# A transformer block in one core: first token tiles of batch 2 and of the MLP prepared inside attention, other tiles on GpSimd's queue

## The chip, the core and the metric

The kernel runs on one core of a Trainium2 chip. The core has a matrix engine (TensorE, PE in the profile; PEld are its weight loads), a vector engine (VectorE, DVE), an engine for functions (ScalarE, ACT), a general one (GpSimd, POOL) and one that only issues transfers (SyncE, SP). Transfers can be issued by SP, ACT and POOL. Each engine works its own instructions off in order and waits at semaphores for the others. The metric is the device time of one execution in microseconds (us); lower is better.

## What is computed

One block of a conditioned transformer on x of 2 batches x 2048 tokens x 576 features, 16 heads of 36, MLP width 2304, all in float32:

```
mod = silu(c) @ w_ada + b_ada                  # six rows of 576 for each batch
xn  = layernorm(x, 1e-6) * (1 + sc_msa) + sh_msa
q, k, v = xn @ w_qkv + b_qkv, by head; q, k = layernorm over the head
o   = softmax(q k^T / sqrt(36)) v
x   = x + g_msa * (o @ w_proj + b_proj)
xn2 = layernorm(x, 1e-6) * (1 + sc_mlp) + sh_mlp
out = x + g_mlp * (gelu(xn2 @ w1 + b1) @ w2 + b2)
```

## The kernel before

With small gains of the head norms (as here) the branch `block_of_small` runs. TensorE's instructions keep the order in which they are written, over the whole branch. Elsewhere a scheduler of the language places the instructions of each engine, and may pull one forward if its inputs are there; inside `tc.manual_schedule(engines=...)` the named engines keep the written order for the instructions of that section. Tiles of a pool have a number of buffers, and a new tile waits until the old one in its buffer is no longer read.

The stages, for each of the two batches:

- **Input stage** (`inputs`): 16 token tiles of 128. A tile is loaded, normalised over its row (`rows_normed`: statistics and normalisation on VectorE, square root on ScalarE), transposed in 32x32 squares on VectorE into the one buffer `squares`, stored as four transfers into a DRAM tile `turned` of 576 x 128 (`tile_turned`), and loaded back with features on partitions (`turned_loaded`: one transfer of 512 features, two of the last 64). ScalarE applies the modulation (`turned_modulated`), GpSimd forms the rest part. `product` multiplies by the weights: four whole chunks of 128 features (L1025) and one of 64 in two rounded parts (L1027). VectorE adds biases and norms the heads. VectorE is in written order here.
- **Attention** (`attend`): 8 head pairs p x 4 query blocks qb x 4 key groups g, 128 steps of about 6 us. A step has score products (L1117), exponentials on ScalarE (L1121) and, one step later, value products (L1130) that VectorE adds up in `ot` (L1176, L1178). `finish` sends the row sums through DRAM, divides, and stores into `qo` (L1155). A dictionary `hooks` puts other work at a step (p, qb, g). The PSUM has eight banks `b`, handed out in turn.
- **Projection** (`outputs`): the PSUM is laid out anew as four tiles `s` of two banks. Four groups of four token tiles: whole chunks of the first two tiles, the last chunk for all four (L423), whole chunks of the other two (L412). VectorE evicts each tile times the gate (L1227) and adds the residual (L1234), which goes to `x1_dram`. The dictionary `between` puts other work before tile t.
- **MLP**, after both batches: first products in a seven-product scheme over 8 token blocks and 9 feature steps (L1494, L1508), gelu, hidden values to DRAM; then the second products (L1645).

In the kernel before, the two first tiles of batch 2 are turned from `between` of the first projection, and the first five of the MLP from that of the second, both with transfers on ACT's queue; the sums and rest parts of w1 are made there too (L1409 to L1412 on VectorE, L406, L407 and L1405 on GpSimd). The second projection and the MLP are one section with VectorE in written order. Other token tiles use SP's queue, but MLP loads use GpSimd's. The w1 loads stand on SP behind the last `qo` stores of attention. The buffer of the transposed tile and the order around it:

```
squares = xs["pool"].tile([P, C], F32, name="squares", bufs=1)
nc.vector.transpose(squares, xt[:, :C])
...
with tc.manual_schedule(engines={mybir.EngineType.DVE, mybir.EngineType.Pool}):
    attend(b, att, hooks)
```

Of the kernel before, what the change touches and what calls it, by code (L numbers as in the profile page):

```python
# [31 lines left out]
def dit_block(  # L32
# [368 lines left out]
    def weight_parts(dst, src, subtract=None):  # L401

        if subtract is None:
            nc.vector.tensor_copy(dst[0:64], src)
        else:
            subtract.tensor_copy(dst[0:64], src)  # L406
        (subtract or nc.vector).tensor_tensor(dst[64:128], src, dst[0:64].bitcast(F32), ALU.subtract)  # L407
# [350 lines left out]
    def block_of_small():  # L758
# [99 lines left out]
        def input_weights(then=lambda t: None):  # L858
            pool, close = opened("wq")
            wq = pool.tile([P, FULL, 3 * C], F32, name="wq")  # L860
            wq4 = pool.tile([P, 3 * C], F32R, name="wq4")
            bq = pool.tile([P, 3 * C], F32, name="bq")
            for f0, n in ((0, HALF), (HALF, HALF), (C, C), (2 * C, C)):
                f = slice(f0, f0 + n)
                nc.sync.dma_start(out=wq[:, :, f], in_=w_qkv[0:512, f].rearrange("(k p) f -> p k f", p=P))
                if f0 == HALF:
                    nc.sync.dma_start(out=bq[0:64, :], in_=w_qkv[512:576, :])
                    weight_parts(wq4, bq[0:64, :])
                if f0 == C:
                    then(1)  # L870
                    nc.sync.dma_start(out=bq, in_=b_qkv.partition_broadcast(P))
                    then(2)
            return (wq, wq4, bq), close
# [12 lines left out]
        def tile_turned(xt, queue):  # L886

            rows_normed(xs["pool"], xt, repeated=False)
            squares = xs["pool"].tile([P, C], F32, name="squares", bufs=1)
            nc.vector.transpose(squares, xt[:, :C])  # L890
            xs["count"] = xs.get("count", 0) + 1
            turned = dram.tile([C, P], F32, name=f"turned{xs['count']}")
            by_square = turned.rearrange("(k d) (g j) -> g d k j", d=SQ, j=SQ)
            for g in range(P // SQ):
                queue.dma_start(
                    out=by_square[g], in_=squares[g * SQ : (g + 1) * SQ, :].rearrange("p (k j) -> p k j", j=SQ)
                )
            return turned

        def turned_loaded(dst, cols, turned, queue):  # L900

            full, _, tail = dst
            queue.dma_start(out=full[:, :, cols], in_=turned[0:512, :].rearrange("(k p) n -> p k n", p=P))
            for r0 in (0, 64):
                queue.dma_start(out=tail[r0 : r0 + 64, :], in_=turned[512:576, :])

        def turned_modulated(dst, cols, which, b):

            full, _, tail = dst
            for k in range(FULL):  # L910
                part = full[:, k, cols]
                nc.scalar.activation(part, part, AF.Identity, **affine(which, k, b))  # L912
            last_modulated(dst, cols, tail, which, b)
# [24 lines left out]
        def inputs(b, weights, work, xnt, rows, loaded):  # L938
# [75 lines left out]
            def next_rows(t):  # L1014
                return tile_turned(loaded.pop(0), nc.sync) if loaded else input_turned(b, t, nc.sync)

            def product(w, xnt):

                ps = s_tile()
                full, parts, _ = xnt  # L1020
                for a in range(2):
                    f = slice(w * C + a * HALF, w * C + (a + 1) * HALF)
                    out_a = ps[:, a, :HALF]
                    for k in range(FULL):
                        nc.tensor.matmul(out_a, full[:, k, :], wq[:, k, f], start=k == 0, stop=False)  # L1025
                    for i in range(2):
                        nc.tensor.matmul(out_a, parts[:, i, :], wq4[:, f], start=False, stop=i == 1)  # L1027
                return ps
# [17 lines left out]
            for t in range(NT - 2):  # L1046
# [4 lines left out]
                if not turning:  # L1051
                    ahead = input_loaded(rows, nc.sync)
                q = product(0, xnt)
                k = product(1, xnt)
                if turning:
                    ahead = second_by_feature(rows)
                else:
                    input_modulated(b, ahead)
# [13 lines left out]
            for t in range(NT - 2, NT):  # L1072
                both = work.tile([P, 2 * C], F32, name="both", bufs=3)
                if t + 1 < NT:
                    ahead = input_loaded(rows, nc.sync)
# [124 lines left out]

        def residual_begun(b, t):
# [77 lines left out]
        for b in range(B):  # L1279
# [44 lines left out]
            }  # L1324
            if b == 0:
# [6 lines left out]
            with tc.manual_schedule(engines={mybir.EngineType.DVE, mybir.EngineType.Pool}):  # L1332
                attend(b, att, hooks)
# [4 lines left out]
            if b + 1 < B:  # L1338
                weights, close_weights = input_weights()
                between = {  # L1340
                    6: [lambda: opening.update(rows=input_turned(b + 1, 0, nc.scalar))],
                    8: [lambda: opening.update(xnt=input_loaded(opening["rows"], nc.scalar))],
                    10: [lambda: opening.update(rows=input_turned(b + 1, 1, nc.scalar))],
                    12: [lambda: input_modulated(b + 1, opening["xnt"])],
                }
                outputs(b, wp, between, spare)
                xnt, rows = opening["xnt"], opening["rows"]
# [47 lines left out]
        nc.sync.dma_start(out=last_rows, in_=w1[512:576, :].rearrange("p (a f) -> p a f", a=2))  # L1395
        for i, (k, f) in enumerate(((0, 0), (0, 1), (1, 0), (1, 1))):
# [3 lines left out]
            )  # L1400
        left, right = last_rows[:, 0], last_rows[:, 1]
        last_parts = [
            lambda: weight_parts(wr[0], left, nc.gpsimd),
            lambda: weight_parts(wr[1], right, nc.gpsimd),
            lambda: nc.gpsimd.tensor_tensor(right, right, left, ALU.subtract),  # L1405
            lambda: weight_parts(wr[2], right, nc.gpsimd),
# [13 lines left out]
        first, between = {}, {}  # L1420
        for j in range(TPB + 1):
            n, i = divmod(j, TPB)
            cols = slice(i * P, (i + 1) * P)
            between.setdefault(2 * j + 6, []).append(lambda n=n, cols=cols: turned_modulated(xnts[n], cols, 2, 0))
            between.setdefault(2 * j + 1, []).append(
                lambda j=j, n=n, i=i: first.update({j: mlp_loaded(n, i, nc.scalar)})
            )
            between.setdefault(2 * j + 3, []).append(
                lambda j=j: first.update({j: tile_turned(first[j], nc.scalar)})
            )  # L1430
            between.setdefault(2 * j + 4, []).append(
                lambda j=j, n=n, cols=cols: turned_loaded(xnts[n], cols, first[j], nc.scalar)
# [102 lines left out]
        def ahead(job):  # L1535
# [11 lines left out]
            if todo := at(-2):  # L1547
                rows_ahead[todo] = tile_turned(rows_ahead[todo], nc.sync)
            for offset in (0, 1):
                if todo := at(offset):  # L1550
                    m, i = todo
                    cols = slice(i * P, (i + 1) * P)
                    if offset == 0:
                        turned_loaded(xnts[m % 2], cols, rows_ahead.pop(todo), nc.sync)
# [20 lines left out]
        for job in range(0, NB * HF, 2):  # L1575
# [3 lines left out]
            ahead(job + 1)  # L1579
            if f1 == 0:  # L1580
                token_sums(n1)
            last_part(n0, f0, 0)
            gelu_stored(n0, f0, 0)
# [149 lines left out]
```

## Time and profile before

| | us |
|---|---|
| median of 3 runs | 3208.73 (3208.04 to 3211.12) |
| profiled execution | 3212.09 |
| its span | 3209.8 |
| TensorE busy in the span | 3164.1 |
| first projection, L412 from 1044.78 to the first product of batch 2's inputs | 71.5 |
| second projection, L412 from 2116.33 to the first MLP product at 2208.85 | 92.5 |
| mean granted TensorE clock | 0.994 |

The span runs from the first to the last instruction of the profiled execution; times in the text count from its start. A busy engine is one with an instruction in work; an idle one waits, and the profile tells what ended the wait. Idle time of an engine costs only where it holds up TensorE.

### The profile page before, as it was taken

How to read it: one execution, taken by the hardware profiler on the slowest of the kernel's cores; microseconds unless marked ns; L12 is line 12 of the kernel's file. 1: busy time of each engine (PE TensorE's matmuls, PEld its weight loads, DVE VectorE, ACT ScalarE, POOL GpSimd, SP SyncE). 2: the span in 40 equal slices, each digit the busy share in tenths (PEclk: the TensorE clock that was granted, in tenths of full speed). 3: DMA queues.
4: the chain of work that ended last, by engine and by line, in shares of the span. 5: the costliest groups of instructions: out<-in, count | busy, mean ns of one | idle time of the engine just before them, and what ended most of it. 6: DMA issues, size and time to landing. Idle time of an engine off the chain costs nothing.

```text
span 3209.8 us, 47255 instructions
## 1 busy us (share of the span) xinstructions
PE 3164.1 (99%) x17833; PEld 1897.9 (59%) x17833; DVE 1506.7 (47%) x2196; ACT 1521.8 (47%) x2954; POOL 398.9 (12%) x503
## 2 busy tenths in 40 slices
PE   8999999999999999999999999989999999999999
PEld 6884333333333788733333333347888888777777
DVE  5784333333333467633333333336566554455454
ACT  2435666666676033466666666623655652000000
POOL 2121000111110111200001111022000000111111
PEclk9999999999999999999999999999999999999999
DMA  5333212223231423221222222147555533333321
GB/s 155 70 72 85 76 36 67 64 74 77 71 90 32 143 58 76 50 57 41 47 50 69 60 72 72 44 150 223 166 134 135 141 108 130 135 133 111 118 104 38
DMA packets 317977, 291.51 MB, mean 91 GB/s; under 512 B 172707, under 2 KB 257132, under 8 KB 315628
## 3 DMA queue, kind: packets, MB, share of 16 engines
q1 hardware_dynamic: 273380, 216.08, 24.0%
q0 software_dynamic: 22640, 66.23, 7.5%
q10 hardware_dynamic: 21720, 6.10, 0.9%
q8 instruction: 143, 2.34, 0.3%
q14 instruction: 94, 0.77, 0.1%
HBM read 155.42 MB, written 84.63 MB: 75 GB/s over the span
## 4 chain that ended last, share of the span: by engine, by line
PE 94%; DMA 2%; DVE 1%; SPq 1%; POOL 1%; issue 0%; ACT 0%; ACTq 0%; DVEq 0%; POOLq 0%
PE b L1130 29%; PE b L1117 19%; PE s L1645 15%; PE m L1494 11%; PE s L1025 10%; PE s L412 2%; PE m L1508 2%; PE one L1494 2%; PE s L1027 1%; PE s L985 1%; DMA x_dram<-x 1%; DMA bq<-in_w_qkv_dram 0%; PE s L423 0%; DMA turned<-squares 0%; DMA xnt<-turned 0%
## 5 line engine op out<-in xcount | busy, mean ns | idle before, releaser
L1121 ACT ACTIVATE pt<-b 128x512 f32<-128x512 f32 x2048 | 1057.6, 608 | 489.6 <-PE b L1130 274.2
L1130 PE MATMUL b<-pt,vt 128*64 128x512 f32 x4096 | 937.4, 600 | 0.0
L1130 PEld LDWEIGHTS b<-pt,vt 128*64 128x64 f32 x4096 | 272.4, 137 | 584.4 <-issue 442.3
L1117 PE MATMUL b<-qm,km 32*128 32x512 f32 x4096 | 571.2, 615 | 0.8 <-DVE vt L1036 0.7
L1178 DVE TENSOR_TENSOR ot<-b,ot 128x512 f32<-128x512 f32 x192 | 132.8, 692 | 653.1 <-PE b L1130 652.7
L1117 PE MATMUL b<-qe,ke 16*128 16x512 f32 x2048 | 425.7, 792 | 0.0
L1025 PE MATMUL s<-wq,xnt 128*128 128x288 f32 x1536 | 406.3, 408 | 1.4 <-ACT xnt L391 0.8
L1117 PEld LDWEIGHTS b<-qm,km 32*128 32x128 f32 x4096 | 193.4, 185 | 271.3 <-ACT pt L1121 208.0
L1645 PE MATMUL s<-ws,as 128*128 128x288 f32 x1440 | 351.8, 406 | 0.0
L1025 PEld LDWEIGHTS s<-wq,xnt 128*128 128x128 f32 x1536 | 281.0, 190 | 63.4 <-ACT xnt L912 1.0
L1645 PEld LDWEIGHTS s<-ws,as 128*128 128x128 f32 x1440 | 273.6, 190 | 75.6
L1149 DVE RECIPROCAL den<-den 128x512 f32<-128x512 f32 x64 | 213.6, 3337 | 11.1 <-DMA den<-den_dram 11.1
L1494 PE MATMUL m<-xnt,wb 128*128 128x256 f32 x864 | 210.3, 379 | 2.0 <-DVE cs L1528 1.1
L1494 PE MATMUL m<-s,wb 128*128 128x256 f32 x864 | 210.0, 379 | 0.0
L1176 DVE COPY ot<-b 128x512 f32<-128x512 f32 x64 | 44.3, 692 | 340.5 <-PE b L1130 340.5
L1494 PEld LDWEIGHTS m<-s,wb 128*128 128x128 f32 x864 | 164.2, 190 | 22.3
L1117 PEld LDWEIGHTS b<-qe,ke 16*128 16x128 f32 x2048 | 109.6, 184 | 114.2 <-issue 112.9
L1494 PEld LDWEIGHTS m<-xnt,wb 128*128 128x128 f32 x864 | 158.9, 190 | 21.5 <-ACT tail L392 1.3
L1532 ACT ACTIVATE cs<-cs,b_sb 128x512 f32<-128x512 f32 x144 | 101.7, 720 | 116.9 <-DVE cs L1527 113.4
L412 PE MATMUL s<-wp,qo 128*128 128x288 f32 x512 | 131.1, 417 | 16.4 <-DVE product L1227 15.6
L1645 PE MATMUL s<-ws,hidden 128*128 128x288 f32 x576 | 142.3, 406 | 0.0
L1623 DVE TENSOR_TENSOR as<-hidden 128x1152 f32<-128x1152 f32 x80 | 138.0, 1787 | 0.0
(181 smaller groups left out, 2638.9 us busy)
## 6 DMA issues: line engine op xcount, KB each, us to landing
gelu<-cs SPq DMA_DIRECT2D x144, 256.0 KB
hidden<-gelu SPq DMA_DIRECT2D x16, 2304.0 KB
den<-den_dram SPq DMA_DIRECT2D x128, 128.0 KB
turned<-squares SPq DMA_DIRECT2D x220, 72.0 KB
xnt<-turned SPq DMA_DIRECT2D x56, 256.0 KB
x_dram<-kr POOLq DMA_DIRECT2D x48, 288.0 KB, 2.8
qm<-qo SPq DMA_DIRECT2D x192, 64.0 KB
kr<-in_x_dram POOLq DMA_DIRECT2D x32, 288.0 KB, 3.8
```

The source lines that it names most:

```text
L412: nc.tensor.matmul(outs[a], stationary(k, a), moving(k, a), start=(first and k == 0), stop=(not first and k == FULL - 1),)
L1025: nc.tensor.matmul(out_a, full[:, k, :], wq[:, k, f], start=k == 0, stop=False)
L1117: nc.tensor.matmul(ps, k[r, keys], q[r, :], start=first, stop=not first)
L1121: nc.scalar.activation(pt[:, h, :], banks[2 * c + h], AF.Exp, scale=SCALE)
L1130: nc.tensor.matmul(acc[64 * h : 64 * h + 64, :], vt[:, v0 : v0 + 64], pt[:, h, :], start=pt is pts[0][0], stop=pt is pts[-1][0],)
L1149: nc.vector.reciprocal(den, den)
L1178: nc.vector.tensor_tensor(ot, acc, ot, ALU.add)
L1494: nc.tensor.matmul(out_m[m], wb[:, slot[m], k, f * P : (f + 1) * P], moving[m](k), start=k == 0 and m in (1, 2, 5, 6), stop=k == 1 and m == 1,
L1508: nc.tensor.matmul(out_m[m], wr[w][:, f * P : (f + 1) * P], a[:, i, t * PAIR : (t + 1) * PAIR], start=False, stop=i == 1 and m != 2,)
L1532: nc.scalar.activation(part, part, AF.Gelu, bias=b1_sb[:, g : g + 1])
L1623: nc.vector.tensor_tensor(stationary[m], x_, y_, op)
L1645: nc.tensor.matmul(ms[m], stationary[m][:, f, :], ws[m][:, f, :], start=(f == 0), stop=(f == HF - 1))
```

## The change

Five things are done.

- The first two tiles of batch 2 and the first five of the MLP are loaded (hook (7, 1, 1)), measured (from (7, 2, 0) on, one a step) and turned (hook (7, 3, 3), the last step) inside attention, by the new `rows_begun`, in parts of the key tile that are free by then. One square root serves all tiles of a group. ScalarE joins VectorE and GpSimd in the written order of attention. From `between` only the modulation stays.
- Other token tiles are loaded, stored turned and loaded back on GpSimd's queue. The MLP's first turned tiles are loaded on SP between the four parts of w1, and w1's last rows come after them.
- The last 64 features are loaded into the rest-part tile itself, not into `tail`; in the MLP `ahead(job + 1)` moves behind `last_part`.
- For the first tile the whole chunks of q and k run before the rounded parts, and the last weight rows come in two transfers and three conversions.
- The rest parts of w1 are made on VectorE, not on GpSimd.

The core of the diff:

```diff
                 if f0 == HALF:
-                    nc.sync.dma_start(out=bq[0:64, :], in_=w_qkv[512:576, :])
-                    weight_parts(wq4, bq[0:64, :])
+                    for w in (slice(0, C), slice(C, 3 * C)):
+                        nc.sync.dma_start(out=bq[0:64, w], in_=w_qkv[512:576, w])
+                    for w in range(3):
+                        w = slice(w * C, (w + 1) * C)
+                        weight_parts(wq4[:, w], bq[0:64, w])
...
         def tile_turned(xt, queue):
-
             rows_normed(xs["pool"], xt, repeated=False)
+            return squares_turned(xt, queue)
+
+        def squares_turned(xt, queue):
+
             squares = xs["pool"].tile([P, C], F32, name="squares", bufs=1)
...
             for r0 in (0, 64):
-                queue.dma_start(out=tail[r0 : r0 + 64, :], in_=turned[512:576, :])
+                queue.dma_start(out=parts[r0 : r0 + 64, 1, cols].bitcast(F32), in_=turned[512:576, :])
...
             def next_rows(t):
-                return tile_turned(loaded.pop(0), nc.sync) if loaded else input_turned(b, t, nc.sync)
+                return tile_turned(loaded.pop(0), nc.gpsimd) if loaded else input_turned(b, t, nc.gpsimd)
...
                 if turning:
+                    q, k = (product(w, xnt, None, (0,)) for w in range(2))
+                    for w, ps in enumerate((q, k)):
+                        product(w, xnt, ps, (1,))
                     ahead = second_by_feature(rows)
                 else:
+                    ahead = input_loaded(rows, nc.gpsimd)
+                    q = product(0, xnt)
+                    k = product(1, xnt)
                     input_modulated(b, ahead)
...
+        def rows_begun(tiles):
+
+            st = xs["pool"].tile([P, 2, 6], F32, name="st", bufs=2)
+            mv = xs["pool"].tile([P, len(tiles), 2], F32, name="mvs", bufs=1)
+            rstd = xs["pool"].tile([P, len(tiles)], F32, name="rstds", bufs=1)
+
+            def load(i):
+                xt, src = tiles[i]
+                not_sooner(xt)
+                nc.gpsimd.dma_start(out=xt, in_=src)
+
+            def measure(i):
+                for a in range(2):
+                    nc.vector.bn_stats(st[:, a, :], tiles[i][0][:, a * HALF : (a + 1) * HALF])
+                nc.vector.bn_aggr(mv[:, i, :], st.rearrange("p a s -> p (a s)"))
+
+            def turn():
+                nc.scalar.activation(rstd, mv[:, :, 1], AF.Sqrt, bias=eps6)
+                nc.vector.reciprocal(rstd, rstd)
+                turned = []
+                for i, (xt, _) in enumerate(tiles):
+                    nc.vector.tensor_scalar(xt, xt, mv[:, i, 0:1], rstd[:, i : i + 1], ALU.subtract, ALU.mult)
+                    turned.append(squares_turned(xt, nc.gpsimd))
+                return turned
+
+            return load, measure, turn
...
+            if b + 1 < B:
+                begun = [(spare[9 + t], x[b + 1, t * P : (t + 1) * P, :]) for t in range(2)]
+            else:
+                begun = [(spare[3 + j], x1_dram[0, j * P : (j + 1) * P, :]) for j in range(TPB + 1)]
...
+            hooks |= {(7, 1, 1): rows_opened, (7, NBLK - 1, NG - 1): rows_turned}
+            hooks |= {
+                (7, 2 + i // NG, i % NG): lambda i=i: opening["begun"][1](i) for i in range(len(begun))
+            }
...
-            with tc.manual_schedule(engines={mybir.EngineType.DVE, mybir.EngineType.Pool}):
+            with tc.manual_schedule(
+                engines={mybir.EngineType.DVE, mybir.EngineType.Pool, mybir.EngineType.Activation}
+            ):
                 attend(b, att, hooks)
...
-                between = {
-                    6: [lambda: opening.update(rows=input_turned(b + 1, 0, nc.scalar))],
-                    8: [lambda: opening.update(xnt=input_loaded(opening["rows"], nc.scalar))],
-                    10: [lambda: opening.update(rows=input_turned(b + 1, 1, nc.scalar))],
-                    12: [lambda: input_modulated(b + 1, opening["xnt"])],
-                }
-                outputs(b, wp, between, spare)
-                xnt, rows = opening["xnt"], opening["rows"]
+                first_turned, rows = opening["turned"]
+                xnt = input_loaded(first_turned, nc.sync)
+                outputs(b, wp, {12: [lambda: input_modulated(b + 1, xnt)]}, spare)
...
-        nc.sync.dma_start(out=last_rows, in_=w1[512:576, :].rearrange("p (a f) -> p a f", a=2))
+        first = opening["turned"]
         for i, (k, f) in enumerate(((0, 0), (0, 1), (1, 0), (1, 1))):
             nc.sync.dma_start(
...
+            for j in (2 * i, 2 * i + 1):
+                if j <= TPB:
+                    n, t = divmod(j, TPB)
+                    turned_loaded(xnts[n], slice(t * P, (t + 1) * P), first[j], nc.sync)
+        nc.sync.dma_start(out=last_rows, in_=w1[512:576, :].rearrange("p (a f) -> p a f", a=2))
         left, right = last_rows[:, 0], last_rows[:, 1]
         last_parts = [
-            lambda: weight_parts(wr[0], left, nc.gpsimd),
+            lambda: weight_parts(wr[0], left),
...
             if todo := at(-2):
-                rows_ahead[todo] = tile_turned(rows_ahead[todo], nc.sync)
+                rows_ahead[todo] = tile_turned(rows_ahead[todo], nc.gpsimd)
...
             whole_part(n0, f0, 0)
-            ahead(job + 1)
             if f1 == 0:
                 token_sums(n1)
             last_part(n0, f0, 0)
+            ahead(job + 1)
```

## The prediction

> **What bounds the kernel now.** I read the page's busy times first, then the waits of TensorE, then the timelines around the longest of them. In the list of waits the columns are who waited, for whom, then total us, times, longest us; in a timeline, start us, us, instruction, and in brackets the idle time just before and what ended it.
>
> ```profile
> PE 3164.1 (99%) x17833; PEld 1897.9 (59%) x17833; DVE 1506.7 (47%) x2196; ACT 1521.8 (47%) x2954; POOL 398.9 (12%) x503
> ```
> ```profile
> PE s L412 <- DVE product L1227: 15.6, 2, 12.3
> ...
> PE b L985 <- ACT pt L1121: 4.0, 1, 4.0
> ...
> PE s L1027 <- DVE wq L407: 1.5, 1, 1.5
> ...
> PE m L1494 <- DVE cs L1528: 1.1, 1, 1.1
> ```
> TensorE is the bound, with 3209.8 - 3164.1 = 45.7 us without work. So only these few places can pay, and a wait put on TensorE is lost in full. The largest is in the second projection, before the MLP:
>
> ```profile
> 2164.60 10.11 PE L412 MATMUL s<-wp,qo 128*128 128x288 f32 x32 [12.28 <-DVE product L1227]
> ...
> 2176.78 8.03 PE L412 MATMUL s<-wp,qo 128*128 128x288 f32 x32
> ```
> ```profile
> 2150.58 0.16 DVE L278 RECIPROCAL rstd<-std 128x1 f32<-128x1 f32 x1 [14.36 <-ACT std L276]
> ...
> 2158.39 0.78 DVE L890 STREAM_TRANSPOSE squares<-x_first 128x576 f32<-128x576 f32 x1 [7.04 <-DMA turned<-squares]
> ```
> VectorE, in fixed order here, stood for the token tiles of the MLP: 14.36 us for a square root of ScalarE, which was itself held by its DMA issues, and 7.04 us until the single squares buffer had been stored. The evictions stood behind. Note the 10.11 us against 8.03 for the same 32 matmuls: after a stop some 2.1 us more are lost.
>
> The second place is the start of attention of batch 1. One line for each stretch (start:end, its us, busy time of PE, PEld, DVE, ACT, POOL, granted clock, DMA share, GB/s): the first two are batch 1 from its last input product to its third group of value products, the third the same of batch 2.
>
> ```profile
> 252.80:269.50 16.70, 12.02 (x55) 7.34 (x54) 4.48 (x11) 11.24 (x23) 5.22 (x7) 0.74 0.47 101
> 269.50:286.60 17.10, 17.05 (x88) 6.38 (x89) 5.15 (x11) 8.48 (x16) 3.17 (x7) 0.86 0.17 30
> 1343.40:1365.40 22.00, 21.95 (x141) 9.86 (x140) 8.88 (x21) 14.98 (x28) 6.41 (x9) 1.00 0.29 53
> ```
> The same work takes 33.8 us and 22.0 us. The chain of waits has the reason: the modulation of batch 2's first tiles, written in the projection but free in order on ScalarE, was pulled forward to here, waits for its tile's DMA, and stands ahead of the first exponentials:
>
> ```profile
> 255.20 2.97 DMA xnt<-turned
> 258.25 0.88 ACT xnt L912 x2
> 259.15 1.28 ACT L1121
> ```
>
> **What the skill says.** "TensorE: Matmul & The Clock Gate", Part 1, says that after an idle window of about 3.4 us the clock falls to half and rises again after about as long of work. The trace agrees: 10.11 - 8.03 = 2.1 us lost after 12.28 us idle. "ScalarE: Activation LUTs", What ACT_TABLE_LOAD costs, gives about 1283 ns for a change of function set; the trace has 1.28 us. "DMA: Bandwidth & Descriptors", Anatomy of one DMA, gives about 2.0 us fixed for a DMA of GpSimd's queue and says that many descriptors can be emitted "before the incremental cost shows up"; here 288 KB from POOL take 0.54 us of issue and land 2.4 us after its start at the least, 2.8 in the median (L1211). No DMA of POOL in this trace has 576 pieces of 128 B, as a store of squares has.
>
> **Part A: nothing of batch 2 is pulled ahead of attention of batch 1.** Its two tiles now depend on hooks in the last attention pair, and ACT too keeps the written order. That stretch should look like batch 2's: 33.8 - 22.0 = 11.8 us. One tile (batch 2's third, the first in the order of its input stage) can still be pulled forward and take a little. I take -11.5; bounds -12 and -4.
>
> **Part B: the turn at the last step of attention.** At hook (7, 3, 3) stand on ACT a table load 1.28 and a Sqrt, on DVE for each tile a normalisation 0.58 and a transposition 0.78, on POOL four stores. Loads and statistics come 4 to 8 steps (6 us each) earlier: POOL is 12% busy and DVE 47%, so 2 and 5 loads at 0.55 and statistics at 1.0 a tile are hidden. But there is one squares buffer: transposition i+1 waits until the four stores of tile i have landed. Call a cycle c = 0.78 + 0.05 + three issues e + the landing of the last, 2.4 + (e - 0.55), so c = 2.7 + 4e. Nearest rows for e: 0.50 us with few rows, 0.54 with 128. From that slope 576 pieces come to some 0.75 (estimate). Bounds: 0.55, and 2.0 if the page's fixed cost were paid by each in turn. I take e = 0.75, c = 5.7.
>
> What is queued behind on DVE is the last addition of attention into ot:
> ```profile
> 2116.47 0.69 DVE L1178 TENSOR_TENSOR ot<-b,ot 128x512 f32<-128x512 f32 x1 [2.77 <-PE b L1130]
> ```
> It frees a PSUM bank that the projection takes over. Banks are handed out in turn, 8: batch 1 asks for 9 (rest of inputs, modulation) + 128 x 8 + 127 = 1160 before the last sum, so bank 0 and projection tile 0; batch 2 for 6 + 1024 + 127 = 1157, so bank 5 and tile 2. The trace agrees: TensorE waits 0.8 us on ot at the first projection and not at all at the second.
>
> Batch 1: the exponentials end at 1041.1; load and Sqrt, reciprocal and normalisation put the first transposition at 1043.5; the second is the only one that waits: ot is added at 1043.5 + 5.7 + 1.5 = 1050.7 against 1044.7 now. TensorE stands for 6.0 more, and 2.1 for the clock: **+8.1**.
>
> Batch 2: exponentials end at 2113.55, first transposition 2116.0, four cycles, then 0.78 + 0.69: ot at 2116.0 + 22.8 + 1.5 = 2140.3. TensorE reaches tile 2 at 2125 and stands some 15 us. After it, 9.1 us of the first group, 2.1 for the clock, three groups of 17.86 (as in batch 1's projection): the projection ends at 2205.1. Now it ends at 2207.9 and the MLP starts at 2208.85 after 0.90 idle: **-3.8**. So the stall of token tiles goes (15.6 idle + 0.9 + two slow starts of 2.1 and 1.7 = 20.3) and another takes most of its place.
>
> Late next there: w1 on SP comes behind the last qo stores, so 12 us after ot instead of at 2132.8; 15 loads of turned tiles (some 1.5 us of SP a tile) and 1.6 MB now lie between the four w1 parts, and last_rows comes last. About 7 MB at the 410 GB/s seen at 2140:2152 is 17 us, so last_rows at about ot + 34; its first use on DVE must be done by ot + 38. It just fits; up to +5 if not. weight_parts now on DVE (about 8 us in all, by L404 and L407 at 1.05 and 1.95 for 1728 columns) lies in the space that 5 tiles x 2.5 leave.
>
> **Part C: the start.** Whole parts of q and k run before the rest parts, so the 1.5 us wait on L407 is covered, and the bias row of weights comes in two pieces. From 20.76 q and k need 8.8 plus 2 for the clock, so 31.6 instead of 34.0; the third weight load, issued after the bias at 25.3, lands near 32. **-2.0**, bounds -0.5 and -3.
>
> **Part D: other tiles on POOL.** A tile costs POOL 0.55 + 4e + 3 x 0.55 = 5.2 us every 14 us in the input stage (227 us for 16 tiles) and less in the MLP; POOL has room, the head scaling of 2.13 stands behind it with an iteration of slack. In the MLP the stores no longer stand behind ws on SP: the 1.1 us wait on cs goes, **-1.1**. The tail tile loaded straight into parts: same counts, 0. Bounds for the rest -2 and +4. ACT in order in attention: only exponentials there, 0.
>
> **Sum:** -11.5 + 8.1 - 3.8 - 2.0 - 1.1 = -10.3, or 5c - 38.8 in general. The profiled execution took 3212.1 (span 3209.8 and 2.3 around it), so 3201.8; the median of runs, 3.4 lower, becomes **3198.4 us**.
>
> **Rivals.**
> 1. POOL's issue of such stores is dear (slower). If e is 2.0, c is 10.7: batch 1 loses 13, the second projection 16, sum +14.7: 3223. It decides from c = 7.8 (e = 1.3); beyond 0.2% from e = 1.6. For it: nothing on POOL shows more than 128 rows. Against: 16 to 128 rows cost only 0.05 us more. 0.28.
> 2. Half of A stays away, because what is pulled forward is replaced by batch 2's third tile: A -6, sum about -5: 3204. For: it was pulled forward before too (a transposition at 254.45). Against: its modulation, which held ACT, can't be. 0.15.
> 3. The turn doesn't hold ot (the order lets the addition pass, or stores land at once): then B is 0 and -21, sum -35: 3173. Against: DVE kept the written order in attention. 0.07.
>
> **How the numbers follow.** Forecast 0.50, nine tenths of it between 3193 and 3202. A difference under 0.2% (6.4 us) can't be told from none by this measurement. Faster: 0.45 of the forecast, 0.02 of rival 2, 0.07 of rival 3; slower: 0.22 of rival 1; the rest, 0.24, is same. The range leaves out rival 3 and the dear end of rival 1: e = 0.55 gives -14.3, with the bounds of C and D 3191; e up to 1.7 gives 3217.
>
> **What would show it.** Right: no L912 before the first exponential at 259, that stretch near 22 us; five transpositions 5 to 6 us apart after the last exponential of batch 2, and TensorE waiting on ot of L1178 at both projections. Wrong: store issues on POOL over 1.3 us; transpositions with no wait between them; waits on last_rows' parts; TensorE idle inside the input stages.

## The result: slower by 0.28%, where a gain of 0.3% was forecast

| | before | after |
|---|---|---|
| median of 8 runs each, us | 3208.39 (3203.93 to 3211.12) | 3218.17 (3210.52 to 3221.34) |
| profiled execution (span), us | 3212.09 (3209.8) | 3216.34 (3214.6) |

The ratio, from all runs together, is 1.0028, with a 95% interval of 1.0017 to 1.0039 (the quotient of the two medians is 1.0030); 3198.4 was forecast, with 3217 as the upper end. The two profiled executions differ by 4.3 us only: that of before lies 3.7 above its median, that of after 1.8 below its own. So what the traces below explain is 4.8 us of span; the other 5 us of the 9.8 are spread of the runs.

The span can be cut at three places at which the same matmul begins:

| stretch, us | before | after | difference | forecast |
|---|---|---|---|---|
| start to first projection | 1044.78 | 1032.38 | -12.4 | -13.5 (A and C) |
| first to second projection | 1071.55 | 1078.55 | +7.0 | +8.1 (B, batch 1) |
| second projection to MLP | 92.52 | 101.12 | +8.6 | -3.8 (B, batch 2) |
| MLP to the end | 1000.95 | 1002.55 | +1.6 | -1.1 (D) |

Three rows are within 3 us of the forecast. The third is 12.4 off, and it alone turns the sign.

TensorE is busy for 3159.8 us in the kernel after, 4.3 less than before, and GpSimd for 673.1 instead of 398.9. The list of waits of TensorE (who waited, for whom, total us, times, longest):

```profile
PE s L420 <- DVE ot L1183: 14.1, 1, 14.1
...
PE s L420 <- DVE product L1259: 7.6, 2, 4.5
PE s L409 <- DVE ot L1183: 4.8, 1, 4.8
PE s L1028 <- ACT xnt L391: 2.7, 1, 2.7
...
PE m L1537 <- DVE cs L1571: 2.3, 2, 1.5
```

The 15.6 us at the evictions that stood behind the token tiles are gone. In their place stand 14.1 and 4.8 us on `ot`, where waits were forecast, and 7.6 us on evictions, which were not. The stretch at the start of attention of batch 1, from its last input product to its third group of value products, took 33.8 us before and takes 22.0 now (250.51 to 272.48). TensorE has no gap there (a window as in the prediction: start:end, us, busy time of PE, PEld, DVE, ACT, POOL, clock, DMA share, GB/s):

```profile
240.00:262.00 22.00, 22.00 (x128) 14.22 (x126) 13.15 (x28) 13.99 (x26) 6.40 (x6) 1.00 0.18 34
```

The chain of waits of the kernel after (start, us, what), from the end of the turn to the MLP, shows what the prediction had to price:

```profile
2131.01 2.15 DMA turned<-squares
2133.29 0.78 DVE squares L893
2134.07 0.59 DVE ot L1183
...
2137.24 3.57 DMA den<-den_dram
2140.83 3.36 DVE den L1154
...
2148.18 0.71 SPq L1160
2148.94 0.53 SPq L908
...
2153.69 26.24 DMA last_rows<-in_w_dram
2179.96 0.76 DVE wr L403
...
2182.13 0.77 DVE product L1259
2182.94 1.33 PE s L420 x4
```

SPq is the transfer queue of SyncE. Read the chain from below. TensorE goes on at 2182.94 after an eviction, which stood behind the conversion of w1's last rows, which took 26.24 us to land after their issue at 2153.69. That issue was the last on SP's queue, behind w1's four parts, the turned tiles (L908) and the `qo` stores (L1160). These waited for the division, that for the row sums, and those for the last addition to `ot`, which stood behind the last transposition.

TensorE's own timeline of this stretch has three long stops, with slow matmuls behind each; the third, 4.51 us, ends at 2182.94 (start, us, instruction, in brackets the wait before it); GpSimd's has the issue of the first residual rows:

```profile
2134.70 1.33 PE L420 MATMUL s<-wp,qo 64*128 64x288 f32 x4 [14.08 <-DVE ot L1183]
...
2157.99 1.62 PE L420 MATMUL s<-wp,qo 64*128 64x288 f32 x8 [3.09 <-DVE product L1259]
2159.55 17.23 PE L409 MATMUL s<-wp,qo 128*128 128x288 f32 x64
...
2184.20 16.85 PE L409 MATMUL s<-wp,qo 128*128 128x288 f32 x64
```
```profile
2149.70 3.23 POOL L1254 DMA_DIRECT2D x<-x_dram  x6
```

The same 64 matmuls take 15.79 us where no stop stands before them (e1, 2119.30).

### The profile page after: what moved, and what is told of

It reads as the page before. It is cut to its first block, busy times and chain, and to the rows that moved or that the text cites. A ratio compares the mean times of both kernels' runs of the same rounds, so it can differ in the third digit from the quotient of the medians.

```text
span 3214.6 us, 47348 instructions
## 1 busy us (share of the span) xinstructions
PE 3159.8 (98%) x17833; PEld 1895.2 (59%) x17833; DVE 1510.3 (47%) x2213; ACT 1515.2 (47%) x2951; POOL 673.1 (21%) x946
## 3 DMA queue, kind: packets, MB, share of 16 engines
q1 hardware_dynamic: 105012, 175.48, 17.9%
q0 software_dynamic: 45328, 112.92, 13.4%
## 4 chain that ended last, share of the span: by engine, by line
PE 95%; DMA 3%; DVE 1%; SPq 0%; ACT 0%; issue 0%; POOL 0%; DVEq 0%; ACTq 0%; POOLq 0%
PE b L1135 28%; PE b L1122 19%; PE s L1688 15%; PE s L1028 11%; PE m L1537 11%; PE s L409 3%; PE m L1551 2%; PE one L1537 2%; PE s L1030 2%; PE s L988 1%; DMA last_rows<-in_w_dram 1%; DMA gelu<-cs 0%; DMA bq<-in_w_qkv_dram 0%; PE s L420 0%; DMA turned<-squares 0%
## 5 line engine op out<-in xcount | busy, mean ns | idle before, releaser
L898 POOL DMA_DIRECT2D turned<-squares x248 | 167.0, 679 | 391.1 <-DVE squares L893 368.4
L915 ACT ACTIVATE xnt<-xnt,mod 128x128 f32<-128x128 f32 x248 | 102.6, 481 | 138.5 <-DMA xnt<-turned 110.8
L1239 POOL DMA_DIRECT2D kr<-in_x_dram x32 | 17.5, 548 | 715.0 <-DVE met L786 700.2
```

The lines of the kernel that those rows point to most:

```text
L898: queue.dma_start(out=by_square[g], in_=squares[g * SQ : (g + 1) * SQ, :].rearrange("p (k j) -> p k j", j=SQ))
```

## Experiments

Theory 1: the single squares buffer makes the turn long, and everything behind it late. Theory 2: w1's last rows and the residual rows land late, and that decides. Theory 3: the other tiles on GpSimd's queue cost by themselves. Theory 4 came after e5: with the single buffer, the whole load phase begins only after the turn. The last column is the time over that of the kernel before, with its 95% interval; the runs of the kernel before were taken together with the experiment's, with a median of 3208.4 to 3210.2.

| run | median, us | ratio to before (95%) |
|---|---|---|
| after | 3218.17 | 1.0028 (1.0017 to 1.0039) |
| e1 own squares | 3196.13 | 0.9956 (0.9943 to 0.9970) |
| e13 two squares buffers | 3202.54 | 0.9981 (0.9973 to 0.9989) |
| e15 two squares buffers, last rows first | 3198.25 | 0.9961 (0.9947 to 0.9974) |
| e5 turn after `ot` | 3217.14 | 1.0029 (1.0020 to 1.0039) |
| e10 e5, loads on ACT's queue | 3221.78 | 1.0042 (1.0028 to 1.0055) |
| e14 e10, residual rows first | 3215.52 | 1.0018 (1.0012 to 1.0025) |
| e2 last rows first | 3212.70 | 1.0012 (1.0004 to 1.0021) |
| e17 sums of w1 two tiles later | 3213.20 | 1.0012 (1.0004 to 1.0020) |
| e3 other tiles on SP | 3216.72 | 1.0024 (1.0014 to 1.0033) |
| e4 kernel before, ACT in order | 3209.05 | 1.0001 (0.9992 to 1.0009) |
| e9 MLP's turn undone | 3201.34 | 0.9980 (0.9971 to 0.9988) |
| e11 e9, own squares | 3196.40 | 0.9961 (0.9947 to 0.9974) |
| e6 e1, w1 on ACT's queue | 3189.27 | 0.9936 (0.9923 to 0.9950) |
| e12 e6, other scratch order | 3193.72 | 0.9955 (0.9941 to 0.9968) |
| e16 e1, turned tiles on ACT's queue | 3194.87 | 0.9954 (0.9940 to 0.9967) |
| e18 e6, sums two tiles later | 3188.01 | 0.9933 (0.9919 to 0.9946) |

### The length of the turn

e1 gives each turned tile a place of its own in the key tile:

```diff
-        def squares_turned(xt, queue):
+        def squares_turned(xt, queue, squares=None):
-            squares = xs["pool"].tile([P, C], F32, name="squares", bufs=1)
+            if squares is None:
+                squares = xs["pool"].tile([P, C], F32, name="squares", bufs=1)
...
+                own = [spare[11], spare[8]]
...
+                own = [*spare[8:12], spare[0]]
...
-                    turned.append(squares_turned(xt, nc.gpsimd))
+                    turned.append(squares_turned(xt, nc.gpsimd, own[i]))
```

> Changed kernel, but each turned tile's transposition goes to squares of its own (free places of kr), so that no transposition in the turn waits for a store. Theory 1 (the single squares buffer holds the last ot addition, and with it the bank, the qo stores and the w1 loads behind them): both waits of TensorE on ot (14.1 and 4.8 us) go, with their slow clock; ot is added 20 us earlier in batch 2; 23 us less than the changed kernel if the two later waits on L1259 (3.1 and 4.5 us) stay, 30 less if they go too: 3188 to 3195. Theory 2 (what decides at the end of attention of batch 2 is that w1's last rows and the residual rows land late): batch 1 wins 7, batch 2 next to nothing, since the wait only moves from ot to L1259: about 3210. Theory 3 (the tiles on GpSimd's queue cost by themselves): the 7 and 16 us are won as in theory 1, but the result stays above the kernel before.

Measured: 22 us below the kernel after. VectorE's timeline in the kernel after, and then in e1:

```profile
2110.63 0.78 DVE L893 STREAM_TRANSPOSE squares<-kr 128x576 f32<-128x576 f32 x1
...
2133.29 0.78 DVE L893 STREAM_TRANSPOSE squares<-kr 128x576 f32<-128x576 f32 x1 [5.33 <-DMA turned<-squares]
2133.99 0.65 DVE L1183 TENSOR_TENSOR ot<-b,ot 128x512 f32<-128x512 f32 x1
```
```profile
2108.90 0.78 DVE L894 STREAM_TRANSPOSE kr<-kr 128x576 f32<-128x576 f32 x1
...
2114.33 0.78 DVE L894 STREAM_TRANSPOSE kr<-kr 128x576 f32<-128x576 f32 x1
2115.03 0.65 DVE L1184 TENSOR_TENSOR ot<-b,ot 128x512 f32<-128x512 f32 x1
```

From the first transposition to the addition it is 23.4 us with one buffer and 6.1 without waits. No wait on `ot` is left at either projection. But the trace of e1 shows a second change, which the edit doesn't ask for: on SP's queue, where the order is free, w1's last rows now go out ahead of w1's parts (`wb`), while in the kernel after they are the last issue.

```profile
2129.30 0.53 SPq L1454 DMA_DIRECT2D last_rows<-in_w_dram  x1
...
2130.21 0.41 SPq L1446 DMA_DIRECT2D wb<-in_w_dram  x1
```

So the 22 us can't be put down to the turn alone. The next run keeps the order of the kernel after.

e13 alternates between two buffers (`own = [None, spare[8]]` and `[None, spare[8], None, spare[8], None]`):

> Changed kernel with two squares buffers for the turn in attention, used in turn (the second in a free place of kr), instead of one. If the turn lasts as long as its stores make it, transposition i waits for the stores of tile i-2: GpSimd's four issues of 0.67 us are then the cycle, 2.7 instead of 5.7 us a tile; ot comes at about 2123 instead of 2134 in batch 2 and without wait in batch 1. Theory 1/4 (everything behind the turn shifts with its length): 7 us in batch 1 and about 11 us in batch 2 less than the changed kernel, 3199, most of the way to the 3196 of squares of their own. If only a turn with no wait at all helps, it stays above 3205.

Measured: 3202.5, 15.6 us below the kernel after; the turn takes 11.6 us (2107.12 to 2118.68), the wait on `ot` is 2.3 us, and the last rows are still the last issue on SP (2149.80). The stop behind them, 4.5 us in the kernel after, has grown; TensorE's line, then VectorE's:

```profile
2169.24 1.33 PE L420 MATMUL s<-wp,qo 64*128 64x288 f32 x4 [11.46 <-DVE product L1260]
```
```profile
2166.26 0.75 DVE L403 CAST wr<-last_rows 64x1152 fp32r<-64x1152 f32 x1 [11.84 <-DMA last_rows<-in_w_dram]
```

So a shorter turn pays, with the order of the loads unchanged, and the last rows cost something of their own. e15 is e13 with the last rows issued ahead of w1's parts:

> Two squares buffers and w1's last rows ahead of w1's parts. With two buffers alone the wait on ot was 2.3 us and TensorE still stopped 11.5 us at an eviction behind the last rows (VectorE 11.8 us at L403). If the order of these loads is a cost of its own, beside the length of the turn, these 11.5 us and some 1.3 of slow clock go: 3202.5 - 12 = 3190 to 3193. If the load phase as a whole is late (some 20 us of transfers at full bandwidth that begin only after the turn), the stop passes to w1's parts and no more than 5 are won: 3197 or more.

Measured: 3198.2, 4 us less, near the second case: the stop passes to w1's parts (TensorE 3.0 + 1.6 + 2.3 us). The order of the loads is worth a few us, here as in e2 below, and so some part of e1's 22 us is likely the order's; the phase as a whole is late.

### Freeing ot alone

e5 calls the turn one step later, after the last addition:

```diff
-            hooks |= {(7, 1, 1): rows_opened, (7, NBLK - 1, NG - 1): rows_turned}
+            hooks |= {(7, 1, 1): rows_opened, (None, None, None): rows_turned}
```

> Changed kernel, but the turn is called one step later, after attention's last addition into ot; it still has the single squares buffer. Theory 1: ot is added at once, so both waits of TensorE on ot go; batch 1 wins 7; in batch 2 VectorE still stands in the turn until about 2134, so TensorE stops some 6 us at the evictions of the first four tiles instead of 15 on ot: 13 to 15 us less than the changed kernel, about 3204. Theory 2: the division by den stands behind the turn as before, so qo, w1 and the last rows are not a bit earlier, and the MLP starts as late as in the changed kernel: only batch 1's 7 us, 3211.

Measured: 3217.1, as the kernel after. Both theories missed. The waits on `ot` are gone, and TensorE's timeline shows what came for them:

```profile
2155.48 2.29 PE L420 MATMUL s<-wp,qo 64*128 64x288 f32 x8 [21.48 <-DVE product L1259]
...
2186.14 1.33 PE L420 MATMUL s<-wp,qo 64*128 64x288 f32 x4 [9.11 <-DVE product L1259]
```
VectorE's timeline has the reasons:
```profile
2135.04 3.31 DVE L1154 RECIPROCAL den<-den 128x512 f32<-128x512 f32 x1
...
2152.36 0.76 DVE L1266 TENSOR_TENSOR x<-x,product 128x576 f32<-128x576 f32 x1 [13.29 <-DMA x<-x_dram]
...
2183.16 0.75 DVE L403 CAST wr<-last_rows 64x1152 fp32r<-64x1152 f32 x1 [18.53 <-DMA last_rows<-in_w_dram]
```

The division still stands behind the turn. The turned tiles' loads too: the first goes out at 2135.18, 0.06 us after the last transposition, and the trace names that transposition as what it waited for. It is the last reader of the key tile there, whose memory is given up before the MLP's tiles are laid out. In the kernel after it is the same (2134.14 after 2134.07). In e13, where the second buffer lies in the key tile, the first of these loads waited for a store out of that tile instead (2122.59). So `ot` was only the first of several things that the turn held. This is theory 4.

e10 moves e5's loads to ACT's queue (in the diff: `nc.sync` to `nc.scalar` for last rows and w1's parts, last rows first, and the first six residual rows from `nc.gpsimd` to `nc.scalar`); e14 issues those residual rows ahead of the others:

> Turn after the last ot addition, single squares buffer as before, and now last rows first, w1's parts and the first six residual rows of batch 2 on ScalarE's queue. The turn after ot alone moved TensorE's stops to L1259: 21.5 us (VectorE in the turn until 2135, then 13.3 us for residual rows) and 9.1 us (18.5 us for the last rows). Theory 4 (what counts is that VectorE and the memory of kr are taken by the turn until 2135, and the loads come only then, in an unlucky order): the loads start at about 2136 instead of 2145, TensorE's first stop shrinks by about 8, the second goes: 15 to 18 us less than with the turn after ot, about 3200, still well above the 3189 with squares of their own. If only the order of the loads counted, both stops would fall to the 6 us of VectorE's own turn: 3192. If the queue doesn't matter, 3217 stays.

> As the turn after ot with the loads on ScalarE's queue (3222, where the residual rows landed behind w1 and TensorE stopped 35.5 us), but the six residual rows first, then the last rows, then w1's parts. If the order of these loads sets the stop, the residual rows are there by about 2145 to 2150, the 35.5 us become 10 to 17, and the time falls by 15 or more to 3200 to 3207. If the residual rows can't start before qo's stores are done, since they lie in ot's memory, and w1 comes later for it, TensorE stops again behind w1's parts and the time stays above 3212.

Measured: 3221.8 and 3215.5. In e10 the residual rows land behind w1, and TensorE stops 35.5 us once; in e14 it stops 16.6 us there, and then 6.3 + 1.6 us behind w1's parts. The stop moves with the order, and the waits at evictions stay between 24 and 37 us in sum (31.4 in e5). All three numbers named for e10 were missed. The first two took the loads to start at about 2136: on ACT's queue, behind the first modulated tile, the last rows went out at 2141 and the residual rows from 2152 on; in e14 w1's parts only from 2158 on. So these two don't show how much an early load phase would give with the single buffer; they show that its order doesn't rescue it. e14 fell into its second case.

### Arrival and due time of w1

e2 takes the kernel after and loads the last rows ahead of w1's parts:

```diff
         last_rows = rows4.tile([64, 2, MH], F32, name="last_rows")
+        nc.sync.dma_start(out=last_rows, in_=w1[512:576, :].rearrange("p (a f) -> p a f", a=2))
         first = opening["turned"]
...
-        nc.sync.dma_start(out=last_rows, in_=w1[512:576, :].rearrange("p (a f) -> p a f", a=2))
```

> Changed kernel, but w1's last rows are loaded first instead of after the four w1 parts and the turned tiles. Theory 1: DVE's 11.3 us at L403 and TensorE's 4.5 us with about 1.1 us of slow clock go, the waits on ot stay: 5 to 6 us less than the changed kernel, 3212. Theory 2: the same place, but the wait passes to the w1 parts that come one load later (L1460): 0 to 3 less. Theory 3: no change.

Measured: 5.5 us less; the interval, 1.0004 to 1.0021, just meets that of the kernel after, but in the trace the stop of 4.5 us is gone, and the one behind the residual rows has grown from 3.1 to 4.9. e17 moves no load, but the due time, in the kernel after:

```diff
-        for i, t in enumerate((6, 8, 10, 12)):
+        for i, t in enumerate((8, 10, 12, 14)):
```

> Changed kernel with the sums and parts of w1 placed two token tiles later in the second projection (tiles 8 to 15 instead of 6 to 13); no load is moved. In the changed kernel the last rows land at 2179.9 and their first use stands ahead of evictions that TensorE needs at about 2176. If that pair of arrival and due time is the cause, TensorE's 4.5 us and 1.1 us of slow clock go, the 3.1 us for residual rows and the 14.1 us on ot stay, and at the end 0 to 3 us come back, since the last sums now lie just before the MLP: 3 to 6 us less than the changed kernel, 3212 to 3215. If the stop was not the last rows' doing, 3218.

Measured: 5.0 us less, within the first case. The stop of 4.5 us is gone, 14.1 and 4.8 on `ot` and 3.7 for residual rows stay. So that stop was arrival against due time of the last rows, as the chain says. The stop behind the residual rows was not tried by itself in the kernel after; that it is theirs is read from VectorE's wait of 7.7 us for them.

### The other parts

e3 puts the other tiles back on SP's queue (`nc.gpsimd` to `nc.sync` in five lines); e4 adds only `mybir.EngineType.Activation` to attention's written order in the kernel before; e9 turns the MLP's five tiles in the second projection again, as the kernel before does, with w1's last rows first and their parts on GpSimd, and keeps batch 2's turn; e11 is e9 with own squares for batch 2's two tiles.

> Changed kernel, but the other token tiles of the input stages and of the MLP use sync's queue again. Theory 1: GpSimd's queue is no cost, the time is within 3 us of the changed kernel, rather above it by 1 (the wait on cs in the MLP). Theory 3: GpSimd's queue costs some 5 us or more over 32 input tiles and 28 MLP tiles, and the time falls by that much.

Measured: 3216.7; its interval overlaps almost wholly with that of the kernel after, and the 5 us or more of theory 3 don't show. Two details of its trace serve below.

> Kernel before, but ScalarE keeps the written order in attention too; nothing else is changed. If part A needs no more than that, the modulation of batch 2's first tile no longer stands ahead of the first exponentials of batch 1 (33.8 us for that stretch becomes 22) and the time falls by 11 us against the kernel before, 3197. If the modulation can still be pulled ahead of attention, since it is written after it and its tile is loaded early, the time stays at 3208.

Measured: no change, the second case. ScalarE's timeline in e4 still has the modulation of batch 2 (L912) ahead of the function table for the first exponentials of batch 1, which is loaded at 258.78:

```profile
257.88 0.88 ACT L912 ACTIVATE xnt<-xnt,mod 128x128 f32<-128x128 f32 x2 [2.75 <-DMA xnt<-turned]
```

> Changed kernel, but the five tiles of the MLP are normed, turned and loaded inside the second projection as in the kernel before, with w1's last rows first and their parts on GpSimd; batch 2's two tiles keep their turn in attention. Theory 1: the end of batch 2's attention costs what it did before (92.5 us from second projection to MLP instead of 101.1), the rest as in the changed kernel: 8 to 9 us less than it, 3208 at most, and 4 us under the kernel before. Part A alone then stands: batch 1's start stays 11 us shorter, its turn costs 7. Theory 3: also slower than before, as the tiles on GpSimd's queue remain.

> Only batch 2's two tiles are turned in attention (MLP's tiles as in the kernel before), and these two have squares of their own. The 5.0 us of TensorE on ot at the first projection and its slow clock go: 6 to 7 us less than with the MLP turn undone (3201.3), 3195. This is the gain of parts A and C with no price for the turn: 12 us under the kernel before. If the wait only moves to the first evictions, 3201 stays.

Measured: 3201.3 and 3196.4. e9 won 17 us over the kernel after, not 8 to 9: its stretch from the second projection to the MLP took 86.9 us, 5.6 less than even before. e11 lies 12.6 us under the kernel before, near the number expected, but that isn't the gain of A and C alone: of the 13.0 us between the two profiled executions 9.9 lie before the first projection, and 5.1 between the second projection and the MLP (87.4 us instead of 92.5); the other two stretches lost 2.1. Between the second projection and the MLP the second of two stops of the kernel before (3.3 us at 2188.14, and the slow matmuls behind it) doesn't come; why was not tried. And e11, which gives up the MLP's turn in attention, is as fast as e1, which keeps it (3196.4 and 3196.1): that turn paid only where w1's loads were moved too, as in e6 below.

### Combinations

e6 issues the last rows, now first, and w1 on ACT's queue, e12 takes other scratch tiles for the residual rows, e16 puts the turned tiles on ACT's queue and leaves w1 on SP's, last rows first; e18 is e6 with e17's edit.

> Squares of their own, and w1's last rows and four parts are issued by ScalarE's queue, which is idle there, last rows first; the turned tiles stay on sync's. The trace with squares of their own still has 3.1 + 2.2 + 1.6 us of TensorE waiting on L1260, behind DVE waits of 10.8 and 6.1 us for w1's parts, and about 2 us of slow clock. If w1's place behind qo's stores and the turned tiles is what is left of the late-loads part, these go: about 8 us less than with the squares alone, 3188. If the parts land no sooner (memory not yet free, or the transfers share the bandwidth), the time stays at 3196.

> Squares of their own and w1 on ScalarE's queue, with the first six residual rows in other places of the scratch memory, so that rows 4 to 6 need not wait 12.8 us. If that wait is for memory under ot, VectorE's 9.2 us at L1267 and with it part of TensorE's 2.1 and 2.4 us go: 2 to 4 us less than 3189. If TensorE's stops come from the division and from w1's second part alone, no change.

> Squares of their own, last rows first, and the five turned tiles loaded by ScalarE's queue, which has nothing to do there, so that w1's four parts follow each other on sync's. If w1's parts are late because turned tiles stand between them, VectorE's waits of 10.8 and 6.1 us for them shrink and TensorE's 3.1 + 2.2 + 1.6 us go with the slow clock: 8 us less than with the squares alone, 3188 or less, as with w1 on ScalarE's queue (3189). If the DMA bandwidth is what is short there, 3194 to 3196 stays.

> Squares of their own, last rows and w1 on ScalarE's queue, and the sums and parts of w1 two token tiles later. There TensorE stopped 2.4 us, with 1.7 us of slow clock, at an eviction behind VectorE's 8.1 us wait for w1's second part, and 2.1 us earlier. If later sums take that wait away, 4 us less than 3189 if nothing comes back at the end: 3185; 3189 if as much comes back before the MLP.

Measured: e6 3189.3, as expected. e12 brought no gain (4.4 us more, with intervals that overlap). e16 won only 1 us over e1, its second case: with nothing between w1's parts on SP their four issues still spread from 2130.7 to 2153.2, with the DMA engines 93% busy and more; in e6 they spread from 2126.1 to 2146.7. e18 3188.0 can't be told from e6, but in its trace TensorE has next to no stop left in this stretch: one of 0.55 us at 2129.79 and one of 0.90 ahead of the MLP. The second projection begins at 2111.12 and the MLP at 2184.77, 73.7 us against 101.1 in the kernel after. e6 and e18 are faster than the kernel before by 0.64 and 0.67%.

## Why the prediction was wrong, step by step

- **Part A** (-11.5): right. Together A and C came to -12.4, and C was 0.9 of it. ScalarE's order alone (e4) did nothing, so the dependence on the hooks is needed; whether it does it without that order was not tried. The rival with half of A did not come.
- **Part C** (-2.0): half of it. q and k did end earlier (30.3 instead of 34.0 us), but then TensorE waited 2.7 us for the second tile's modulation, so the same input product begins at 38.01 instead of 38.90. q and k ended even sooner than priced (31.6); the step that failed is to take their end for the gain: of what comes behind, only the third weight load was looked at.
- **Part B, the cycle** (5.7 us, e = 0.75): right in its make-up, and its size in part by luck. The transpositions follow at 5.4, 5.3, 5.4 and 6.6 us, 5.7 in the mean. An issue takes 0.67 us, and with that the working's sum gives the 5.4 of the first three; the fourth has a pause of 1.23 us in front of its last issue, for which the trace names no cause. The exponentials end at 2108.15, `ot` is added 26.5 us later (26.75 by the working). The rival with a dear issue (e above 1.6) is refuted, though the time went where it said.
- **Part B, batch 1** (+8.1): near in size, +7.0, but two errors offset each other. TensorE waited 4.80 us instead of 0.82 on `ot`, where 6.0 more were worked out, and 32 matmuls took 10.76 us instead of 8.03 (TensorE, then VectorE, then GpSimd):

```profile
1032.38 4.15 PE L409 MATMUL s<-wp,qo 128*128 128x288 f32 x16
1041.33 6.61 PE L409 MATMUL s<-wp,qo 128*128 128x288 f32 x16 [4.80 <-DVE ot L1183]
```
```profile
1039.92 0.78 DVE L893 STREAM_TRANSPOSE squares<-kr 128x576 f32<-128x576 f32 x1 [6.63 <-DMA turned<-squares]
```
```profile
1036.35 2.00 POOL L898 DMA_DIRECT2D turned<-squares  x3 [2.54 <-issue]
```

The second transposition came 7.9 us after the first (1032.05), not 5.7, since GpSimd paused 2.54 us behind the first store, again with no cause named. On the other side the sum lay in the bank of tile 1, not of tile 0, so 16 matmuls (4.15 us) went ahead of the wait. In e3 the pause falls into batch 2 instead: the two transpositions of batch 1 follow at 5.4 us, and the wait is 2.3. In batch 2 of the kernel after the bank was that of tile 3 instead of tile 2, which changes little.

- **Part B, batch 2** (-3.8): wrong, +8.6. The step that failed is "Late next there", which ends "It just fits; up to +5 if not". It set the last rows at `ot` + 34 and their due time at `ot` + 38. They were ready on VectorE at 2179.96, `ot` + 45.3. w1's first part was issued at `ot` + 15.6 (12 were priced) and the last rows at `ot` + 19.0, and these took 26.2 us more to land. For the transfers 17 us were priced, for 7 MB at 410 GB/s; between 2150 and 2180 10.4 MB were moved, and 5.0 of them, residual rows and stores on GpSimd's queue, were not in the sum. That gave a stop of 4.5 us, and the matmuls behind it took 1.8 longer (the granted clock was 0.51 to 2184.20 and 0.71 to 2188). These are the waits on the last rows' parts that the prediction named as a sign of being wrong. A second load was not priced at all: the residual rows of batch 2, on POOL's queue behind the turn's stores and behind GpSimd's subtractions, issued only at 2149.70. Their stop was 3.1 us, with 1.9 of slow matmuls behind it. With a third stop of 0.4 these make up the 11.7 us by which the stretch behind `ot` is longer than worked out (77.4 us; 64.8 were worked out, and 0.9 of idle time ahead of the MLP, which the sum let go without a reason and which every trace still has).
- **Why the working saw so small a risk.** The working took the turn to hold `ot` and asked whether w1 would still fit. The runs show a chain, not a single stop: the turn holds `ot`, the division, the `qo` stores, the memory of the key tile and so the load phase, which then takes some 30 us (2150 to 2180 in the kernel after, 2134 to 2166 in e13). Take one link out (e5) and the next one costs the same; shorten the turn (e13 with the same order of loads, e1) and all of it moves. That memory is given up late was read from the traces; it was not tried by itself.
- **Part D** (-1.1): +1.6 in the profile. The step that failed is that the wait on `cs` goes once the stores leave SP's queue: it became 2.3 us in two pieces. In e3, with these tiles on SP, it is 0.4, and in the traces of the kernels with them on GpSimd 1.4 to 3.2. So the reason given for D does not hold; in the medians e3 can't tell this from nothing.
- **The level.** 3.4 us were taken off since the profiled execution lay above its median. The profile after lies 1.8 below its own; so of the 19.8 us by which the median was missed, about 5 are not in the two profiles. One execution can't give a median to better than that.

## What to carry to other kernels

A step that is moved to the end of a stage must be priced by everything that its engines and its memory hold back, down to the next stage's loads: follow the chain until a transfer that doesn't depend on it, and count what other queues move in the same stretch. If taking one wait away changes nothing, look for the engine or the memory that is held as a whole. Where several transposed tiles are stored one after another, two buffers instead of one, the second in memory that is free only for a short time, were worth 15.6 us here; one for each tile was worth 22, with one load moved ahead besides.

## What the hardware showed

The line of GpSimd's transfer queue (queue, packets, MB, share of 16 engines) before and after:

```profile
q0 software_dynamic: 22640, 66.23, 7.5%
```
```profile
q0 software_dynamic: 45328, 112.92, 13.4%
```

The transfers of the token tiles, stores of 128-byte pieces above all, make far fewer packets on GpSimd's queue: 22,700 more there, 168,000 fewer on SP's (273,380 and 105,012), at the same 291.5 MB in all; with the tiles back on SP (e3) there are 302,458 packets instead of 150,585. That hardly makes the DMA engines less busy (24.0, 7.5 and, on ACT's queue, 0.9% of their time before; 17.9 and 13.4% after), and the time with and without it is the same (e3). The price on POOL is 0.67 us for such a store, against 0.54 for one of 128 rows. And an issue isn't always short: in the second projection of e9, with the DMA engines full (376 GB/s from 2128 to 2146), one of the four stores of a tile took 13.1 us to issue on ACT's queue, and the square root behind it waited 19.3 us; the shortest of the four took 0.34 us.

A stop of TensorE need not be long to cost slow matmuls, and need not cost them. After stops of 2.30 us (e15, at 2175.07) and 2.35 us (e6, at 2166.92) the granted clock was 0.67 and 0.64 for the next 3.3 us, and 32 matmuls took 9.72 us instead of 8.03. After a stop of 2.28 us (e13, at 2119.39) it was 1.00.
